# Half of the in-place scans of a selective-scan kernel take their decays from SBUF in place of PSUM

## The chip, the cores and the metric

The kernel runs on one core of a Trainium2 chip. The metric is the device time of one execution in microseconds (us). Before the change the median of three runs is 11,285.59 us, from 11,276.82 to 11,286.57. The profile comes from one execution of its own, told of below. Engines are named as in the profile: PE (TensorE), PEld (its weight loads), DVE (VectorE), ACT (ScalarE), POOL (GpSimd) and SP (SyncE, which here issues all DMAs).

## The reference, cut to what matters

Eight images of 96 channels, 64 by 64, go through a block with four selective scans, then a small attention and a feed-forward part. The scans are most of the work. Each of four directions (row order and column order, each forwards and backwards) has 192 channels with 16 states each, and 4,096 positions in a row:

```python
def step(hst, inp):
    u_i, dt_i, b_i, c_i = inp
    dA = jnp.exp(dt_i[..., None] * A)
    hst = dA * hst + (dt_i * u_i)[..., None] * b_i[:, :, None, :]
    y = jnp.einsum('bkdn,bkn->bkd', hst, c_i)
    return (hst, y)
...
return ys.transpose(1, 2, 3, 0) + D[None, :, :, None] * u
```

So each position needs a decay dA (an exponential), an input (a product), the recurrence itself, a product with c and a sum over the 16 states. The four directions' results are added up.

## The kernel before

**Chunks and slots.** A direction of an image is cut into 8 chunks of 512 positions, a "unit"; 8 images x 4 directions x 8 chunks are 256 units, worked one after another. A unit has 192 x 16 rows, which are 24 scans of 128 rows (64 channels with 2 states): six tiles (n = 0 to 5) of four scans (m = 0 to 3). One scan is one "slot", q = 24 x unit + 4n + m.

**One slot.** ACT makes the decay (line 1080) of 128 x 512 in a PSUM bank "da", of which there are three. DVE runs the scan (line 1145) over the decay and the input hb, which POOL made in SBUF (line 959: b times du, four scans in one instruction of 128 x 2048). There are two sorts:
- In a *banked* scan the states go back into the PSUM bank in the decay's place. DVE then multiplies them by c into hb (line 1147), and ACT copies the last column to the carry (line 1148).
- In the others the states go into SBUF, in the input's place, hb. One copy of ACT takes the carries of a whole tile (line 1153), and POOL multiplies the tile's states by c (line 965).

`BANKED` says how many scans of each tile are banked: all four of tiles 0, 2 and 4, none of 1 and 3, and one or two of tile 5. So 10 or 11 of the 24 scans of a unit are in place: slots 4 to 7, 12 to 15 and the last two or three.

**Order.** Every engine takes its instructions in the order in which the program gives them out, slot after slot. `plan` lists what else goes out at each slot: inputs of the tile after next (slots 1, 5, 9, 13, 17, 21), outputs (slots 8 and 16, and slot 0 of the next unit), the step sizes (PE, three of ACT, one of DVE at line 938, one of POOL at line 941), their spreading over partitions by DMA, loads of b and c. `decays(q + 2)` gives out the decay of the scan two slots ahead; three banks hold the decay in use and the two next.

**Sums.** PE adds the 16 states with a constant matrix into two PSUM banks (`sums`, line 985). For the last part it adds what the earlier directions left: `before` (line 967) loads that into the SBUF buffers u0 and u1 at slot 0 of the next unit, and the matmul of line 994 adds it at slot 6. `gather` copies the sums (slots 10 and 11) to buffers yt0 and yt1 and asks for a DMA to DRAM that goes out three slots later.

**Beside the scans** run side streams, given out step by step between the slots: the front part of the next image and the back part of the last one, whose operations are spread over PE, ACT, DVE and, for one add, POOL (line 802). One of DVE's is the scaled identity of line 694, once for each image.

Of the kernel before, what the change touches and what calls it, by code (L numbers as in the profile page):

```python
# [9 lines left out]
F32 = mybir.dt.float32  # L10
F16 = mybir.dt.float16
F8 = mybir.dt.float8e5
AF = mybir.ActivationFunctionType
# [9 lines left out]
T = 512  # L23
NC = L // T
G = 4
# [7 lines left out]

BANKED = ((4, 0, 4, 0, 4, 1), (4, 0, 4, 0, 4, 2))

HOLD = 3
LAND = 11
SETTLE = 12
# [5 lines left out]
def kernel(ctx: ExitStack, tc: tile.TileContext, a, out):  # L44
# [9 lines left out]
    P = 128  # L54
# [6 lines left out]
    BANKS = {"da": 3, "dt": 1, "f0": 1, "f1": 1, "y01": 1, "y2": 1}  # L61

    def bank(tag, name):
        return psum.tile([P, T], F32, tag=tag, name=name, bufs=BANKS[tag])


    ident = wp.tile([P, P], F32, name="ident")
# [39 lines left out]
    def into(t, src):  # L107
        nc.sync.dma_start(t, src)
        return t
# [3 lines left out]
    def later(dst, src):  # L113

        requests.append((clock[0] + HOLD, dst, src))

# [6 lines left out]
    def load(name, shape):  # L123
        return into(wp.tile(shape, F32, name="w_" + name), a[name])
# [31 lines left out]
    a_neg = load("a_logs", [P, 4, 3, 8])  # L156
# [23 lines left out]
    dd_a, dd_b = wp.tile([P, P], F32, name="dd_a"), wp.tile([64, 64], F32, name="dd_b")  # L180
# [170 lines left out]
    def scanned(ap):  # L351
        return ap.rearrange("p (h j i) -> p h j i", h=8, j=8)

    def transposed(ap):

        return ap.rearrange("p (w i j) -> p w j i", w=8, i=8)

    def to_columns(t, c):

        return t.rearrange("d (w h e) -> d h w e", w=8, h=8)[:, c]  # L360

    def by_window(ap):
        return ap.rearrange("p (w e) -> p w e", w=8)
# [453 lines left out]
    def in_turn(stages, k, settle):  # L817

        for stage, cs in stages:
            yield from stage(k, cs)  # L820
            if settle:
                yield from settled()
# [12 lines left out]
    def drained(*streams):  # L835
        while any(s.on for s in streams):
            tick()
            for s in streams:
                s.run()

    def all_issued():
        drained(Stream(iter((HOLD + 1,))))

# [11 lines left out]
    units, images = [], []  # L855
    for b in range(out.shape[0]):
# [3 lines left out]
        for order, (pair, back) in enumerate((p, k) for p in s["pairs"] for k in range(2)):  # L860
            for i in range(NC):
                u = Unit()
# [11 lines left out]
    first = front(0, images[0])  # L874
# [9 lines left out]
    sp = scan_pool.enter_context(tc.tile_pool(name="scan", bufs=2))  # L884
# [70 lines left out]
    def inputs(u, n):  # L955

        g, j = TILES[n]
        hb = u.hb[n] = sp.tile([P, G, T], F32, tag="hb", name="hb", bufs=HB)
        nc.gpsimd.tensor_tensor(hb, u.bc[0, g], u.du[j].unsqueeze(1).to_broadcast([P, G, T]), ALU.mult)  # L959
# [7 lines left out]
    def before(u):  # L967

        src = u.s["y" if u.order else "u"][u.pair]
        u.plain = []  # L970
        for i, rows in enumerate((slice(0, P), slice(P, src.shape[0]))):
            t = sp.tile([P, T], F32, tag=f"u{i}", name=f"u{i}", bufs=1)[: rows.stop - rows.start]
            u.plain.append(into(t, src[rows, bass.ts(u.c, T)]))

    def sums(u, ns, m):

        if ns[0] == 0 and m == 0:
            u.p = (bank("y01", "p01"), bank("y2", "p2"))
        low, up = slice(0, 64), slice(64, P)
        if len(ns) == 2:  # L980
            todo = [(u.p[0][low], ns[0], m), (u.p[0][up], ns[1], m)]
        else:
            todo = [(u.p[1][low], ns[0], 2 * m), (u.p[1][up], ns[0], 2 * m + 1)]
        for ps, n, i in todo:
            nc.tensor.matmul(  # L985
                ps, halves, u.hb[n][:, i, :], start=TILES[n][0] == 0 and m == 0, stop=False, skip_group_check=True
            )
        if ns[-1] == 5 and m == 1:
            first = u.order == 0
            for ps, w, x in (  # L990
                (u.p[0], dd_a if first else ident, u.plain[0]),
                (u.p[1][low] if first else u.p[1], dd_b if first else ident, u.plain[1]),
            ):
                nc.tensor.matmul(ps, w, x, start=False, stop=True, skip_group_check=True)  # L994

    def gather(u, i):

        ps, d = u.p[i], slice(P * i, P * i + P)
        t = sp.tile([ps.shape[0], T], F32, tag=f"yt{i}", name="yt", bufs=1)

        other = (u.pair, 1 - u.pair, u.pair, 0)[u.order]
        dst = u.s["y"][other][d]
        if other != u.pair:
            nc.scalar.copy(transposed(t), scanned(ps))
            later(to_columns(dst, u.c), by_window(t))
        else:
            nc.scalar.copy(t, ps)
            later(dst[:, bass.ts(u.c, T)], t)
        if u.order == 3 and i == 1:
            if other == u.pair:  # L1010
                u.s["done"].add(u.c)
            elif u.c == (0 if u.back else NC - 1):
                u.s["done"].update(range(NC))

    def plan(u, last, nxt, third):
# [6 lines left out]
        if last:  # L1022
            put(0, outputs, last, 5)
            put(0, before, last)
            for m in range(2):
                put(m, sums, last, (3, 4), 2 + m)
            for m in range(2):
                put(5 + m, sums, last, (5,), m)
            put(7, states, u, 1, 1)
            put(10, gather, last, 0)  # L1030
            put(11, gather, last, 1)
# [38 lines left out]
    def at_index(i):  # L1070
        return units[i] if 0 <= i < len(units) else None

    def decays(q):

        if q >= 24 * len(units):
            return
        u, (n, m) = units[q // 24], divmod(q % 24, G)
        g, j = TILES[n]
        da[q] = bank("da", "da")
        nc.scalar.activation(  # L1080
            da[q], u.delta[j], AF.Exp, scale=a_neg[:, u.k, j, g * G + m : g * G + m + 1]
        )

    da, kept, side, carry = {}, [], [], None
# [13 lines left out]
        step_sizes(units[1:2], i)  # L1098
    inputs(units[0], 0)
    inputs(units[0], 1)  # L1100
    decays(0)
    decays(1)

    def advance(n):

        tick()
        for st in side[:]:
            st.run()

    for u in units:  # L1110
        last, nxt, third = (at_index(u.i + d) for d in (-1, 1, 2))
        if u.new:
            drained(*side)
            b = u.s["b"]
            side = []
            if b == 0:
                side.append(Stream(behind(kit_2, pairs[3:])))
            else:
                side.append(Stream(chain((SETTLE,), in_turn(back_end(b - 1, last.s), kit_b, False))))
            if b + 1 < out.shape[0]:  # L1120
                side.append(Stream(in_turn(front(b + 1, images[b + 1]), kit_f, True), PACE))
            else:
                final = back_end(b, u.s)
                last_kit = back_kit(None, "f0", True, kit_f)
                side.append(Stream(final[0][0](last_kit, range(1, NC)[::-1])))
        if u.i == pairs[3] - 2:
            drained(side[0])
        if third and third.new:
            drained(*side[-1:])
            all_issued()  # L1130
        if u.start:
            carry = sp.tile([P, 24], F32, tag="carry", name="carry")
        todo = plan(u, last, nxt, third)
        for slot in range(24):
            n, m = divmod(slot, G)
            g, j = TILES[n]
            q, hb, first_at = 24 * u.i + slot, u.hb[n], 0 if u.back else T - 1
            col = carry[:, 8 * j + g * G + m : 8 * j + g * G + m + 1]
            while kept:
                kept.pop(0)()  # L1140
            decays(q + 2)
            d = da.pop(q)
            banked = m < u.banked[n]
            dd, x = (d[:, ::-1], hb[:, m, ::-1]) if u.back else (d, hb[:, m, :])
            nc.vector.tensor_tensor_scan(dd if banked else x, dd, x, 0.0 if u.start else col, ALU.mult, ALU.add)  # L1145
            if banked:
                nc.vector.tensor_tensor(hb[:, m, :], d, u.bc[1, g][:, m, :], ALU.mult)  # L1147
                kept.append(lambda col=col, d=d, at=first_at: nc.scalar.copy(col, d[:, at : at + 1]))  # L1148
            elif m == G - 1:
                lo = 8 * j + g * G  # L1150
                kept.append(
                    lambda c=carry[:, lo + u.banked[n] : lo + G].unsqueeze(2), h=hb[:, u.banked[n] :, :], at=first_at:
                    nc.scalar.copy(c, h[:, :, at : at + 1])  # L1153
                )
            for f, args in todo[slot]:
                f(*args)
            place[0] = slot
            advance(slot)
# [7 lines left out]
    for m in range(2):  # L1166
        sums(u, (5,), m)
    gather(u, 0)
    gather(u, 1)
    all_issued()  # L1170
# [77 lines left out]
```

## Time and profile before

| | us | where from |
|---|---|---|
| median of three runs | 11,285.59 | times |
| the profiled execution | 11,276.69 | times |
| its span, first to last instruction | 11,274.7 | profile |
| first scan starts | 299.2 | trace |
| last scan ends | 11,035.9 | trace |
| POOL: inputs of the scans, line 959, 1,536 of them | 6,938.6 | groups |
| POOL: outputs, line 965, 768 of them | 2,984.6 | groups |
| DVE: scans into PSUM, line 1145, 3,087 with a carry | 3,950.2 | groups |
| DVE: scans in place, line 1145, 2,289 with a carry | 2,781.6 | groups |
| DVE: products of the banked scans, line 1147, 3,528 | 2,440.8 | groups |
| ACT: decays, line 1080, 6,144 | 4,216.2 | groups |

How to read it: the first part of the profile's page gives each engine's busy time, the share of the span and the number of instructions. The second cuts the span into 40 slices and gives each slice's busy share in tenths (9 is 90% or more). A row of the groups has the line, the engine, the operation, what it writes and reads, the shape and the count; then the busy time in us and the mean of one in ns; then the idle time of the engine just before these instructions, and what ended it. A row of the waits has who waited for whom, the total in us, how many times, and the longest. A row of the timeline has the start and the duration in us.

### The profile page before, as it was taken

How to read it: one execution, taken by the hardware profiler on the slowest of the kernel's cores; microseconds unless marked ns; L12 is line 12 of the kernel's file. 1: busy time of each engine (PE TensorE's matmuls, PEld its weight loads, DVE VectorE, ACT ScalarE, POOL GpSimd, SP SyncE). 2: the span in 40 equal slices, each digit the busy share in tenths (PEclk: the TensorE clock that was granted, in tenths of full speed). 3: DMA queues.
4: the chain of work that ended last, by engine and by line, in shares of the span. 5: the costliest groups of instructions: out<-in, count | busy, mean ns of one | idle time of the engine just before them, and what ended most of it. 6: DMA issues, size and time to landing. Idle time of an engine off the chain costs nothing. (4 is left out here: it accounts for less than half of the span.)

```text
span 11274.7 us, 97032 instructions
## 1 busy us (share of the span) xinstructions
PE 8525.3 (76%) x23270; PEld 2313.7 (21%) x23270; DVE 10391.9 (92%) x10868; ACT 7482.6 (66%) x14899; POOL 10398.6 (92%) x2782
## 2 busy tenths in 40 slices
PE   6677668887788877888678886788767887676677
PEld 1121112222122211222112221222212221111112
DVE  0999999999999999999999999999999999999993
ACT  2666666767666676667766676666766667666674
POOL 0999999999999999999999999999999999999991
PEclk8787778888788877889788887888878887777778
DMA  3788888988888888888888888889888888888883
GB/s 76 195 200 196 200 190 208 215 219 203 199 208 214 217 194 210 208 210 219 195 208 212 213 215 193 217 200 226 209 199 209 213 221 199 194 198 196 202 201 91
DMA packets 1095376, 2253.25 MB, mean 200 GB/s; under 512 B 435993, under 2 KB 436698, under 8 KB 963731
## 3 DMA queue, kind: packets, MB, share of 16 engines
q1 hardware_dynamic: 1094803, 2247.05, 82.1%
q8 instruction: 184, 3.01, 0.1%
q14 instruction: 389, 3.19, 0.1%
HBM read 1507.14 MB, written 336.69 MB: 164 GB/s over the span
## 5 line engine op out<-in xcount | busy, mean ns | idle before, releaser
L959 POOL TENSOR_TENSOR hb<-b,du 128x2048 f32<-128x2048 f32 x1536 | 6938.6, 4535 | 27.0 <-DMA du<-ua 17.0
L1080 ACT ACTIVATE da<-delta,w_a_logs 128x512 f32<-128x512 f32 x6144 | 4216.2, 689 | 693.1 <-DVE hb L1145 570.8
L985 PE MATMUL p<-hb,halves 128*64 128x512 f32 x12288 | 3788.4, 724 | 787.4 <-POOL hb L965 368.5
L1145 DVE TENSOR_TENSOR_SCAN da<-da,carry,hb 128x512 f32<-128x512 f32 x3087 | 3950.2, 1280 | 52.8 <-ACT da L1080 48.9
L965 POOL TENSOR_TENSOR hb<-hb,c 128x2048 f32<-128x2048 f32 (+2 forms) x768 | 2984.6, 3886 | 296.8 <-ACT carry L1153 252.9
L1145 DVE TENSOR_TENSOR_SCAN hb<-da,carry,hb 128x512 f32<-128x512 f32 x2289 | 2781.6, 1265 | 63.6 <-ACT da L1080 62.6
L1147 DVE TENSOR_TENSOR hb<-da,c 128x512 f32<-128x512 f32 x3528 | 2440.8, 692 | 153.9 <-DVE da L1145 0.5
L1148 ACT COPY carry<-da 128x1 f32<-128x1 f32 x3528 | 554.8, 157 | 2337.9 <-DVE hb L1147 2327.3
L985 PEld LDWEIGHTS p<-hb,halves 128*64 128x64 f32 x12288 | 911.3, 161 | 3513.9 <-issue 2095.9
L435 PE MATMUL conv<-f0im,taps 97*128 97x512 f32 (+1 forms) x2088 | 913.0, 670 | 93.3 <-ACT f0pre L491 54.0
L1145 DVE TENSOR_TENSOR_SCAN da<-da,hb 128x512 f32<-128x512 f32 x441 | 537.7, 1219 | 28.3 <-POOL hb L959 27.3
L941 POOL TENSOR_TENSOR ua<-nat,ua 128x512 f32<-128x512 f32 x256 | 327.4, 1279 | 203.0 <-DMA ub<-u 203.0
L924 PE MATMUL dt<-dts,dt_w 7*64 7x512 f32 (+1 forms) x1024 | 451.1, 662 | 15.8 <-DVE nat L938 12.6
L994 PE MATMUL p<-u,ident 128*128 128x512 f32 x768 | 436.2, 695 | 8.8 <-DMA u<-y 8.8
L938 DVE SCALAR_TENSOR_TENSOR nat<-dt,nat 128x512 f32<-128x512 f32 x384 | 259.6, 676 | 184.4 <-ACT nat L936 184.4
L435 PEld LDWEIGHTS conv<-f0im,taps 97*128 97x128 f32 (+1 forms) x2088 | 256.2, 175 | 683.5 <-issue 523.9
L1145 DVE TENSOR_TENSOR_SCAN hb<-da,hb 128x512 f32<-128x512 f32 x327 | 377.9, 1204 | 4.9 <-ACT da L1080 4.9
L376 PE MATMUL ctr<-f1e,cen_c 96*96 96x512 f32 x402 | 234.7, 693 | 137.4 <-DVE f1e L770 98.6
L382 PE MATMUL var<-f1e,ones_c 96*96 96x512 f32 x350 | 210.8, 687 | 146.3 <-ACT f1e L379 131.7
L619 PE MATMUL cab<-f1im,cab_w 97*32 97x512 f32 x1044 | 272.3, 642 | 14.7 <-DVE f1pad L598 7.8
L1153 ACT COPY carry<-hb 128x4 f32<-128x4 f32 (+2 forms) x768 | 146.8, 191 | 196.1 <-DVE hb L1145 184.1
L656 PE MATMUL cab<-f1m,cab_w 96*96 96x512 f32 x348 | 205.2, 717 | 93.1 <-ACT f1e L665 42.1
(427 smaller groups left out, 7512.6 us busy)
## 6 DMA issues: line engine op xcount, KB each, us to landing
b<-xd SPq DMA_DIRECT2D x1024, 512.0 KB
c<-xd SPq DMA_DIRECT2D x1024, 512.0 KB
delta<-nat SPq DMA_DIRECT2D x1536, 128.0 KB
du<-ua SPq DMA_DIRECT2D x1024, 128.0 KB
y<-yt SPq DMA_DIRECT2D x512, 256.0 KB
u<-y SPq DMA_DIRECT2D x384, 256.0 KB
ua<-u SPq DMA_DIRECT2D x256, 256.0 KB
du<-ub SPq DMA_DIRECT2D x512, 128.0 KB
```

The lines of the kernel that those rows point to most:

```text
L435: nc.tensor.matmul(ps, taps[:, t, lo : lo + n], im[:, r0 + dy : r0 + dy + 8, dx : dx + HW], start=t == 0, stop=t == 8,)
L619: nc.tensor.matmul(ps[at : at + 32, :], cab1_w[:, t, :], k.im.t[:, 8 * q + dy : 8 * q + dy + 8, dx : dx + HW], start=t == 0, stop=t == 8, ...
L924: nc.tensor.matmul(ps, dt_w[32 * w.k : 32 * w.k + R + 1, d], w.dts, start=True, stop=True)
L941: nc.gpsimd.tensor_tensor(x, u.nat, x, ALU.mult)
L959: nc.gpsimd.tensor_tensor(hb, u.bc[0, g], u.du[j].unsqueeze(1).to_broadcast([P, G, T]), ALU.mult)
L965: nc.gpsimd.tensor_tensor(hb, hb, u.bc[1, TILES[n][0]][:, lo:, :], ALU.mult)
L985: nc.tensor.matmul(ps, halves, u.hb[n][:, i, :], start=TILES[n][0] == 0 and m == 0, stop=False, skip_group_check=True)
L994: nc.tensor.matmul(ps, w, x, start=False, stop=True, skip_group_check=True)
L1080: nc.scalar.activation(da[q], u.delta[j], AF.Exp, scale=a_neg[:, u.k, j, g * G + m : g * G + m + 1])
L1145: nc.vector.tensor_tensor_scan(dd if banked else x, dd, x, 0.0 if u.start else col, ALU.mult, ALU.add)
L1147: nc.vector.tensor_tensor(hb[:, m, :], d, u.bc[1, g][:, m, :], ALU.mult)
L1148: kept.append(lambda col=col, d=d, at=first_at: nc.scalar.copy(col, d[:, at : at + 1]))
```

## The change

The decays of the in-place scans with even m go into a new SBUF tile "das" with two buffers: slots 4, 6, 12, 14 and 22, in both rows of `BANKED`. They are 5 of the 24 decays of a unit, 1,280 of 6,144. All others stay in the three PSUM banks. `ahead` holds two lists of the decays still to make, one for PSUM and one for SBUF, each in the scans' order. At each slot q, `decays(q)` gives out from each list as many as there is room for (three in PSUM, two in SBUF, with the one in use counted) and as lie at most eight slots ahead.

To make room, the buffers yt0 and yt1 go away: `gather` copies the sums into u0 and u1, which held what was just added. `before` now keeps whole tiles of 128 rows, of which the first direction uses the lower 64 for the second bank.

```diff
+AHEAD = 8
...
-            t = sp.tile([P, T], F32, tag=f"u{i}", name=f"u{i}", bufs=1)[: rows.stop - rows.start]
-            u.plain.append(into(t, src[rows, bass.ts(u.c, T)]))
+            t = sp.tile([P, T], F32, tag=f"u{i}", name=f"u{i}", bufs=1)
+            into(t[: rows.stop - rows.start], src[rows, bass.ts(u.c, T)])
+            u.plain.append(t)
...
-                (u.p[1][low] if first else u.p[1], dd_b if first else ident, u.plain[1]),
+                (u.p[1][low], dd_b, u.plain[1][low]) if first else (u.p[1], ident, u.plain[1]),
...
-        ps, d = u.p[i], slice(P * i, P * i + P)
-        t = sp.tile([ps.shape[0], T], F32, tag=f"yt{i}", name="yt", bufs=1)
+        ps, d, t = u.p[i], slice(P * i, P * i + P), u.plain[i]
...
+    ahead = ([], [])
+    for q in range(24 * len(units)):
+        n, m = divmod(q % 24, G)
+        ahead[int(m >= units[q // 24].banked[n] and m % 2 == 0)].append(q)
+
     def decays(q):
 
-        if q >= 24 * len(units):
-            return
+        for which, room in ((0, BANKS["da"]), (1, 2)):
+            while ahead[which] and sum(used == which for _, used in da.values()) < room:
+                nxt = ahead[which][0]
+                if nxt > q + AHEAD:
+                    break
+                ahead[which].pop(0)
+                decay(nxt, which)
+
+    def decay(q, which):
+
         u, (n, m) = units[q // 24], divmod(q % 24, G)
         g, j = TILES[n]
-        da[q] = bank("da", "da")
+        da[q] = bank("da", "da") if which == 0 else sp.tile([P, T], F32, tag="das", name="das"), which
         nc.scalar.activation(
-            da[q], u.delta[j], AF.Exp, scale=a_neg[:, u.k, j, g * G + m : g * G + m + 1]
+            da[q][0], u.delta[j], AF.Exp, scale=a_neg[:, u.k, j, g * G + m : g * G + m + 1]
         )
...
-    decays(0)
-    decays(1)
+    decays(-1)
...
-            decays(q + 2)
-            d = da.pop(q)
+            decays(q)
+            d, _ = da.pop(q)
```

## The prediction

> **What bounds the kernel now.** I read the page's busy times first, then its slices, the groups, the waits, and last the timeline around one odd instruction.
>
> ```profile
> PE 8525.3 (76%) x23270; PEld 2313.7 (21%) x23270; DVE 10391.9 (92%) x10868; ACT 7482.6 (66%) x14899; POOL 10398.6 (92%) x2782
> DVE  0999999999999999999999999999999999999993
> POOL 0999999999999999999999999999999999999991
> ```
>
> DVE and POOL are both full from the second slice to the next to last. The first scan starts at 299.2 us and the last ends at 11035.9, so 10,737 us hold the 256 chunks, 41.95 each. In that stretch DVE is busy 10,316 and POOL 10,372: idle 421 and 365 us. Neither can lose or gain much without the other.
>
> ```profile
> L959 POOL TENSOR_TENSOR hb<-b,du 128x2048 f32<-128x2048 f32 x1536 | 6938.6, 4535 | 27.0 <-DMA du<-ua 17.0
> L1080 ACT ACTIVATE da<-delta,w_a_logs 128x512 f32<-128x512 f32 x6144 | 4216.2, 689 | 693.1 <-DVE hb L1145 570.8
> L1145 DVE TENSOR_TENSOR_SCAN hb<-da,carry,hb 128x512 f32<-128x512 f32 x2289 | 2781.6, 1265 | 63.6 <-ACT da L1080 62.6
> L965 POOL TENSOR_TENSOR hb<-hb,c 128x2048 f32<-128x2048 f32 (+2 forms) x768 | 2984.6, 3886 | 296.8 <-ACT carry L1153 252.9
> ```
>
> POOL's work is long multiplies, each with two SBUF inputs. The waits that more decays ahead could remove are small:
>
> ```profile
> DVE hb L1145 <- ACT da L1080: 67.5, 93, 3.0
> DVE da L1145 <- ACT da L1080: 48.9, 22, 6.4
> ```
>
> 116 us in 115 waits: the most that the look-ahead itself can win.
>
> **What the change puts at stake.** Until now every two-input DVE operation of the scan phase has one tensor in PSUM. The change gives 5 scans of each 24 (slots 4, 6, 12, 14, 22), 1,280 in all, both tensors in SBUF. No row shows that beside POOL, so I bound it by the nearest ones:
>
> ```profile
> L1145 DVE TENSOR_TENSOR_SCAN hb<-da,carry,hb x2289: 1250/1260/1285, 346.2 to 11034.7; 128x512 f32<-128x512 f32 x191
> L667 DVE TENSOR_REDUCE totals<-f1e x58: 655/672/683, 2201.7 to 11154.5; 96x1 f32<-96x512 f32 x58
> L694 DVE TENSOR_SCALAR dgate<-ident,gate x8: 268/2484/2492, 2300.0 to 11160.0; 96x96 f32<-96x96 f32 x8
> ```
>
> These columns are least, median and most ns. A scan with one SBUF input never stretches beside POOL (1250 to 1285), nor does a reduction with one SBUF stream (655 to 683). The scaled identity of line 694, SBUF to SBUF, takes 268 ns once POOL has finished and about 2,484 the seven times POOL works. The timeline, DVE's row first and POOL's below, shows why:
>
> ```profile
> 2299.99 2.48 DVE L694 TENSOR_SCALAR dgate<-ident,gate 96x96 f32<-96x96 f32 x1
> 2302.40 1.21 DVE L1145 TENSOR_TENSOR_SCAN hb<-da,hb 128x512 f32<-128x512 f32 x1
> ...
> 2293.42 8.99 POOL L959 TENSOR_TENSOR hb<-b,du 128x2048 f32<-128x2048 f32 x2
> ```
>
> POOL ends at 2302.41, line 694 at 2302.47. All seven end 63 to 70 ns behind a POOL multiply: DVE stood still until POOL's whole instruction was over. So one end is "as L667": no cost. The other is "as L694": each changed scan waits for the multiply in flight. I take L694, because the changed scan draws a second SBUF stream, one more than any row shows running freely; both ends stay in the range.
>
> The Trainium skill, page "SBUF — State Buffer", section "Who interferes with whom", speaks against this change: a DVE instruction with two SBUF inputs contends with a GpSimd instruction that reads SBUF, and whoever comes second is blocked for the whole instruction. L694 agrees with the blocking (2,484 against 268 ns), while two SBUF inputs are not in this trace. By that rule the sum below stands; without it, the free-scan rival's.
>
> **The sum, stage by stage.** POOL's queue per chunk is: after slot 23 an output (L965), an input (L959), the 128x512 multiply of L941, an input; after slot 7 an output and two inputs; after slot 15 the same. Each output waits for the four scans of its tile. Pitches, start to start: L959 and the full L965 4.49 (two in 8.99 to 9.05, less one of 4.53), L941 1.23, the short L965 2.55 on average (200 of 2.31, 56 of 3.41), in-place scan 1.22 (four in 4.80 to 4.92). From a tile's last scan to its output on POOL at the earliest: 0.74 (0.66 to the end of the carry copy of L1153, mean of 768, and 0.08 on). Line 694 needs 268 ns alone but ends at most 70 ns behind POOL, so POOL lets go about 0.2 before its recorded end: DVE gets in between two back-to-back multiplies, and POOL then waits for the scan.
>
> Stage A (slot 23's scan to slot 7's, today 13.76). Slot 4's scan comes 13.76 − 4 × 1.22 = 8.88 into it. POOL's gap before its last input is at 0.74 + 2.55 + 4.49 + 1.23 − 0.2 = 8.81. In the trace 43% come later. Early: scan to 10.03, input to 14.52, slot 6's scan starts at 14.32, and with slot 7's ends at 16.76. Late: it waits for the last input, 13.30, and four scans end at 18.18, without a further wait as POOL has run dry. Mean 17.37, +3.61.
>
> Stage B (to slot 15, today 13.69). Gap at 0.74 + 2 × 4.49 − 0.2 = 9.52; 22% come later. Early 9.52 + 1.22 + 4.49 − 0.2 + 2.44 = 17.47, late 0.74 + 13.47 − 0.2 + 4.88 = 18.89. Mean 17.78, +4.09.
>
> Stage C (to slot 23, today 14.50). Only slot 22 changes: 0.74 + 13.47 − 0.2 + 2 × 1.22 = 16.45, +1.95.
>
> Sum 9.65 us a chunk, × 256 = 2,470. POOL becomes late by this and then waits for DVE; the stages hold both. The rest, at nothing:
> - Look-ahead: the 116 us lie inside stages that POOL's queue now ends. Without that cover it is −116.
> - Decays: still 6,144 activations, 1,280 into SBUF. Nearest rows: SBUF to SBUF 617 (L934) and 709 (L936) against 689, so −92 to +26 us on ACT, which is idle 3,433 us in the phase.
> - Scan reading SBUF for PSUM: the only sign is 1282 against 1260 when the output moves so. Up to −28 us, covered as above; no row shows a loss.
> - Sums copied into u0/u1: the same 512 copies (578 and 1,091 ns). New is that the load of line 973 waits on SP for the write out of that buffer; behind it are dts, the spreads and the states. From the write's issue to the next such load lie 16 us (median of 510); the longest issue of such a write was 4.53. I take 0. If it were 4.5 late at each column-wise chunk (72), 324 us on SP, still under the five slots until the sums read it.
>
> The profiled run took 11,276.7 us (span 11,274.7), 9 under the median 11,285.6. 11,277 + 2,470 = 13,747, rounded to **13,750**.
>
> **Rivals.**
> - *POOL wins every gap* (8%). Back-to-back multiplies overlap by some 45 ns in the timeline, which speaks for it; L694's early release against. Then A is always 18.18, B 18.89, C 16.45: 53.52, +11.57 × 256 = 2,962, **14,240**. With today's leftovers of POOL's instruction at slots 4, 12, 22 (1.11, 2.02, 2.70) and 3.27 at 6 and 14 simply added, 12.37 × 256 gives 14,440, my upper end.
> - *Only POOL waits, or both share finely* (14%). L694's wait is DVE's, against it; but that operation is another kind. 1,280 × 1.25 = 1,600 on POOL, less its 365 idle at best: **12,510 to 12,880**.
> - *Free scans* (13%, the other side). The second stream costs nothing, as L667; then the 116 us of decay waits and the 28 go, and POOL's idle of 365 leaves room: 11,133 to 11,277, say **11,190**. It decides as soon as the wait per changed scan is under 116 / 1,280 = 0.09 us. A page of the skill leans this way: "Perfetto Trace Analysis", section "Optimizing Scalar/DVE Operations", has about 60 ns of access overhead for DVE on SBUF and 125 on PSUM; by it, as an estimate, another 83 us, unseen here.
> - *The change does not get ahead* (3%, no change). Against: slot 12's decay is issued at slot 5, slot 28's at 20, when their delta has long been there.
>
> My forecast keeps 62%. **Range** 12,500 to 14,450: from POOL-only waiting to the added leftovers. It leaves out the free scans, the no-change case and a few per cent beyond. Differences under 0.2% (23 us) can't be told from none. Slower 0.62 + 0.08 + 0.14 = 0.84, same 0.03, faster 0.13.
>
> **What would show it.** The 1,280 scans with SBUF decays should have a median of several us and end with a POOL multiply, while scans from PSUM keep 1.26 to 1.28; POOL's share in the scan phase falls to some 78% (10,372 of 13,208), or stays near 90% if its blocked time is recorded as busy, with idle before L965 for the carry; DVE's waits for decays vanish. If the new scans take 1.2 us and POOL's multiplies stretch to 5.7, POOL alone pays. If neither stretches, I am wrong.

## The result, and the profile after

The changed kernel takes 13,759 us in the median of four runs (13,757 to 13,768), against 11,282 for the kernel before in four runs: a ratio of 1.2197, 95% interval 1.2176 to 1.2218. The forecast was 13,750. The profiled execution took 13,760.1 us with a span of 13,758.4.

The page of the changed kernel, busy times and two rows of slices:

```profile
PE 9199.2 (67%) x23270; PEld 2431.8 (18%) x23270; DVE 13020.8 (95%) x10868; ACT 7572.5 (55%) x14899; POOL 10816.5 (79%) x2782
DVE  1999999999999999999999999999999999999994
POOL 1888888888888888888788888888878888888872
```

DVE looks busier than ever: 13,021 us in place of 10,392 for the same 10,868 instructions. That is not work: as the groups show, the wait sits inside the durations of the changed scans. POOL fell from 92% to 79%. The groups of the changed kernel:

```profile
L960 POOL TENSOR_TENSOR hb<-b,du 128x2048 f32<-128x2048 f32 x1536 | 7298.2, 4766 | 18.1 <-DMA du<-ua 16.9
L966 POOL TENSOR_TENSOR hb<-hb,c 128x2048 f32<-128x2048 f32 (+2 forms) x768 | 2975.7, 3875 | 2022.7 <-ACT carry L1167 1879.3
L1159 DVE TENSOR_TENSOR_SCAN hb<-das,carry,hb 128x512 f32<-128x512 f32 x1120 | 3734.7, 3335 | 0.4
L1159 DVE TENSOR_TENSOR_SCAN hb<-da,carry,hb 128x512 f32<-128x512 f32 x1169 | 1466.5, 1255 | 0.8
```

The 1,120 changed scans with a carry take 3,335 ns in the mean, the in-place scans whose decays stayed in PSUM 1,255. All 1,280 changed ones add up to 4,273 us, where the same slots took 1,614 before: 2,659 more, against 2,481 by which the scan phase grew (13,218 for 10,737). POOL's outputs, which hardly waited before (297 us), now stand idle for 2,023 us until a tile is scanned and its carry copied.

The forms of the scan line in the changed kernel (least, median and most ns):

```profile
L1159 DVE TENSOR_TENSOR_SCAN da<-da,carry,hb x3087: 1254/1281/1293, 340.5 to 13511.3; 128x512 f32<-128x512 f32 x193
L1159 DVE TENSOR_TENSOR_SCAN hb<-da,carry,hb x1169: 1248/1251/1284, 351.6 to 13514.4; 128x512 f32<-128x512 f32 x195
L1159 DVE TENSOR_TENSOR_SCAN hb<-das,carry,hb x1120: 1249/3456/8934, 349.1 to 13513.2; 128x512 f32<-128x512 f32 x187
```

Only the form with both tensors in SBUF stretches, and its least is 1249. Of the 192 changed scans under 1.4 us, 187 began with POOL idle or within 0.3 us of the end of its instruction: there the second SBUF tensor costs nothing extra. DVE's timeline in one chunk of the changed kernel:

```profile
6000.85 4.29 DVE L1159 TENSOR_TENSOR_SCAN hb<-das,carry,hb 128x512 f32<-128x512 f32 x1
6005.06 1.25 DVE L1159 TENSOR_TENSOR_SCAN hb<-da,carry,hb 128x512 f32<-128x512 f32 x1
...
6014.58 2.17 DVE L1159 TENSOR_TENSOR_SCAN hb<-das,carry,hb 128x512 f32<-128x512 f32 x1
6016.67 1.25 DVE L1159 TENSOR_TENSOR_SCAN hb<-da,carry,hb 128x512 f32<-128x512 f32 x1
6017.85 4.30 DVE L1159 TENSOR_TENSOR_SCAN hb<-das,carry,hb 128x512 f32<-128x512 f32 x1
```

and POOL's in the same stretch:

```profile
5998.62 5.43 POOL L960 TENSOR_TENSOR hb<-b,du 128x2048 f32<-128x2048 f32 x1
6006.68 4.51 POOL L966 TENSOR_TENSOR hb<-hb,c 128x2048 f32<-128x2048 f32 x1 [2.62 <-ACT carry L1167]
6011.15 9.91 POOL L960 TENSOR_TENSOR hb<-b,du 128x2048 f32<-128x2048 f32 x2
```

POOL's input ends at 5998.62 + 5.43 = 6004.05, the scan that began at 6000.85 ends at 6005.14, 1.09 later. The median over each of the five changed slots is 1.08. A scan needs some 1.26, so it gets going 0.18 us before POOL's recorded end. The other direction shows too: 408 of POOL's 1,536 input multiplies last over 5 us, mostly 5.4 in place of 4.5, and 402 of them begin inside a changed scan's recorded time (some 360 us in all, 7,298 against 6,939 in the groups). The 9.91 of the last row are two multiplies, one of them so stretched, with a scan between them.

One multiply does not explain the longest scans (8.93 us in the row above, 9.18 without a carry). In 59 of the 1,280 changed scans, 45 of them at slot 4, two to four of POOL's instructions end inside the recorded time; these scans take 6.23 us in the mean. One such scan, and POOL's instructions in its time:

```profile
5013.12 7.91 DVE L1159 TENSOR_TENSOR_SCAN hb<-das,carry,hb 128x512 f32<-128x512 f32 x1
```

```profile
5008.67 4.50 POOL L960 TENSOR_TENSOR hb<-b,du 128x2048 f32<-128x2048 f32 x1
5013.14 1.15 POOL L803 TENSOR_TENSOR f1e<-f1e,f1o 96x512 f32<-96x512 f32 x1
5014.25 1.26 POOL L942 TENSOR_TENSOR ua<-nat,ua 128x512 f32<-128x512 f32 x1
5015.47 4.49 POOL L960 TENSOR_TENSOR hb<-b,du 128x2048 f32<-128x2048 f32 x1
```

Here POOL keeps its turn at three ends in a row, and the scan ends 1.07 us behind the fourth. Why POOL keeps its turn in some places and DVE gets in at others is not shown.

Means of the three stages in us (from last scan to last scan of tiles 1, 3 and 5, in the traces; they move by 0.01 with the first and last chunk):

| stage | before | forecast | after |
|---|---|---|---|
| A, to slot 7 | 13.76 | 17.37 | 17.45 |
| B, to slot 15 | 13.69 | 17.78 | 17.34 |
| C, to slot 23 | 14.50 | 16.45 | 16.87 |
| a chunk | 41.95 | 51.60 | 51.66 |

### The profile page after: what moved, and what is told of

The parts are those of the page before. It is cut to its first block, busy times and chain, and to the rows that moved or that the text cites. A ratio compares the mean times of both kernels' runs of the same rounds, so it can differ in the third digit from the quotient of the medians.

```text
span 13758.4 us, 96349 instructions
## 1 busy us (share of the span) xinstructions
PE 9199.2 (67%) x23270; PEld 2431.8 (18%) x23270; DVE 13020.8 (95%) x10868; ACT 7572.5 (55%) x14899; POOL 10816.5 (79%) x2782
## 5 line engine op out<-in xcount | busy, mean ns | idle before, releaser
L960 POOL TENSOR_TENSOR hb<-b,du 128x2048 f32<-128x2048 f32 x1536 | 7298.2, 4766 | 18.1 <-DMA du<-ua 16.9
L987 PE MATMUL p<-hb,halves 128*64 128x512 f32 x12288 | 4055.3, 771 | 1201.3 <-POOL hb L966 536.7
L1095 ACT ACTIVATE da<-delta,w_a_logs 128x512 f32<-128x512 f32 x4864 | 3356.9, 691 | 1169.4 <-DVE hb L1159 1057.6
L1159 DVE TENSOR_TENSOR_SCAN hb<-das,carry,hb 128x512 f32<-128x512 f32 x1120 | 3734.7, 3335 | 0.4
L1095 ACT ACTIVATE das<-delta,w_a_logs 128x512 f32<-128x512 f32 x1280 | 915.3, 715 | 1557.0 <-DVE hb L1159 1555.1
L1159 DVE TENSOR_TENSOR_SCAN hb<-da,carry,hb 128x512 f32<-128x512 f32 x1169 | 1466.5, 1255 | 0.8
L436 PE MATMUL conv<-f0im,taps 97*128 97x512 f32 (+1 forms) x2088 | 987.2, 728 | 227.2 <-ACT f0pre L492 111.3
L925 PE MATMUL dt<-dts,dt_w 7*64 7x512 f32 (+1 forms) x1024 | 493.2, 716 | 74.8 <-DVE nat L939 71.5
L1159 DVE TENSOR_TENSOR_SCAN hb<-das,hb 128x512 f32<-128x512 f32 x160 | 538.2, 3364 | 0.0
L942 POOL TENSOR_TENSOR ub<-nat,ub 128x512 f32<-128x512 f32 x128 | 162.0, 1266 | 407.9 <-DVE nat L939 378.3
```

The lines of the kernel that those rows point to most:

```text
L436: nc.tensor.matmul(ps, taps[:, t, lo : lo + n], im[:, r0 + dy : r0 + dy + 8, dx : dx + HW], start=t == 0, stop=t == 8,)
L925: nc.tensor.matmul(ps, dt_w[32 * w.k : 32 * w.k + R + 1, d], w.dts, start=True, stop=True)
L942: nc.gpsimd.tensor_tensor(x, u.nat, x, ALU.mult)
L987: nc.tensor.matmul(ps, halves, u.hb[n][:, i, :], start=TILES[n][0] == 0 and m == 0, stop=False, skip_group_check=True)
L1095: nc.scalar.activation(da[q][0], u.delta[j], AF.Exp, scale=a_neg[:, u.k, j, g * G + m : g * G + m + 1])
```

## The experiments

Experiments 1, 11 and 12 have several runs and an interval, the others a single run each; between single runs, differences of a fifth of a per cent are not read.

**1. The shared sum buffers alone.** The decays stay as before. This part of the change is kept, with the whole tiles of `before` that it needs:

```diff
-        ps, d = u.p[i], slice(P * i, P * i + P)
-        t = sp.tile([ps.shape[0], T], F32, tag=f"yt{i}", name="yt", bufs=1)
+        ps, d, t = u.p[i], slice(P * i, P * i + P), u.plain[i]
```

> The part of the change that copies the sums into u0 and u1, alone; all decays stay in PSUM as before. My theory (the whole loss is DVE's wait for POOL at the scans with two SBUF inputs): no difference, 11,282 within 25 us, POOL and DVE both some 97% busy in the scan phase. Rival (SP is held up by the load that now waits for the write out of the same buffer): up to 324 us more, 11,300 to 11,600, with waits of SP at the load of u.

Measured: 11,284 us in ten runs, ratio 1.000, interval 0.999 to 1.001. The load that waits for the write costs nothing. All of the loss lies in the decays.

**2. and 3. What POOL reads.** In the changed kernel and in the kernel before, POOL's input and output multiplies become memsets, so both kernels leave the products with b, du and c out:

```diff
-        nc.gpsimd.tensor_tensor(hb, u.bc[0, g], u.du[j].unsqueeze(1).to_broadcast([P, G, T]), ALU.mult)
+        for _ in range(2):
+            nc.gpsimd.memset(hb, 0.5)
...
-        nc.gpsimd.tensor_tensor(hb, hb, u.bc[1, TILES[n][0]][:, lo:, :], ALU.mult)
+        for _ in range(2):
+            nc.gpsimd.memset(hb, 0.5)
```

> The changed kernel with each of POOL's input and output multiplies (lines 960 and 966) replaced by two memsets of the same tile, which read nothing from SBUF; the inputs of the scans are then a constant, and the products with b, du and c are left out. From the 128x528 memset of 0.53 us I estimate 4.1 us for the two, so POOL is nearly as busy as before. Theory (it is the second SBUF stream that collides with POOL's reads): changed scans of 1.25 us beside POOL's memsets, a few longer ones beside the multiplies of line 942, time 11,050 to 11,300. Rival (DVE waits whatever POOL does, as it would if the write side collided too): changed scans of 2 to 5 us, time above 12,000. The Trainium skill, page SBUF - State Buffer, section Who interferes with whom, says of two-SBUF-input DVE instructions that they contend with a GpSimd instruction that reads SBUF, not with one that only writes it; by that the first of the two holds.

> The same memsets in the kernel before, as the control of the changed kernel with memsets: POOL's multiplies by b, du and c are left out. DVE bound, 11,050 to 11,300. The difference between the two is what the look-ahead and the SBUF decays are worth by themselves when nothing collides: by the 116 us of waits for decays, the changed one is 0 to 150 us faster than this one.

Measured: 11,287 us with the change, 11,279 without. The changed scans with memsets beside them, and then the group of those memsets:

```profile
L1161 DVE TENSOR_TENSOR_SCAN hb<-da,carry,hb x1169: 1247/1258/1284, 342.4 to 11038.1; 128x512 f32<-128x512 f32 x195
L1161 DVE TENSOR_TENSOR_SCAN hb<-das,carry,hb x1120: 1250/1274/3267, 341.2 to 11036.9; 128x512 f32<-128x512 f32 x187
```

```profile
L961 POOL MEMSET hb<- 128x2048 f32 x3072 | 5514.5, 1805 | 115.1 <-PE p L989 26.5
```

POOL works for 8,371 us of the scan phase, less than the 10,372 before but still 78% of it, and writes the same buffers, yet the median changed scan takes 1,274 ns. The collision is with POOL's *reads*. The few long ones, up to 3.3 us, are 15% of those at slot 4, where POOL's queue still has the multiply of the step sizes, which reads. The Trainium skill, page "SBUF — State Buffer", section "Who interferes with whom", says this of instructions with two SBUF inputs, and the run agrees: 3,335 ns beside reading multiplies, 1,308 beside memsets, in the mean.

The pair gives two more answers. The look-ahead and the SBUF decays were expected to be worth 0 to 150 us where nothing collides; no gain is measured (11,287 against 11,279, too close to tell apart). Some collisions are left, though: the scans at the five slots add up to 1,659 us with the change and 1,613 without, nearly all of the 46 us at slot 4. Less these, the change could be worth some 40 us at most, as an estimate. And POOL had been 97% busy in the scan phase before, but with 2,000 us of its work gone the time stays 11,279: POOL does not set it. DVE, busy 10,298 of the phase's 10,728 us there, is the nearest bound.

**4. and 5. The length of the instruction in flight.** POOL's inputs in two halves, in the changed kernel and in the one before:

```diff
-        nc.gpsimd.tensor_tensor(hb, u.bc[0, g], u.du[j].unsqueeze(1).to_broadcast([P, G, T]), ALU.mult)
+        for h in (slice(0, 2), slice(2, 4)):
+            nc.gpsimd.tensor_tensor(
+                hb[:, h, :], u.bc[0, g][:, h, :], u.du[j].unsqueeze(1).to_broadcast([P, 2, T]), ALU.mult
+            )
```

> The changed kernel with each of POOL's input multiplies split into two of 128x1024. The instruction in flight is then at most some 2.3 us long. My theory (a changed scan waits for the whole instruction in flight): the changed scans fall to a mean near 2.1 us, the longest mostly under 3.7, and the time to 12,100 to 12,600, although POOL has more instructions. Rival (a price of the scan itself, or of bytes moved in SBUF): scans stay at 3.3 us and the time at 13,760 or above, by POOL's 0.13 us for each split.

> The same split in the kernel before, as the control. No scan there has two SBUF inputs, so only POOL's second instruction counts: 2 x 2.31 - 4.49 = 0.13 us for each of 1,536, 200 us at most: 11,280 to 11,480 under every theory, scans unchanged at 1.25 to 1.28 us.

Measured: 12,651 us with the change, 11,328 without. The changed scans with halved inputs:

```profile
L1162 DVE TENSOR_TENSOR_SCAN hb<-das,carry,hb x1120: 1251/2132/9349, 354.6 to 12407.5; 128x512 f32<-128x512 f32 x187
```

The median falls from 3,456 to 2,132 and the time by 1,108 us, though POOL has 1,536 more instructions: the price is mostly the multiply in flight. The time is 50 above the range and the mean of all changed scans 2.45 in place of 2.1. The theory left out the scans that sit through more than one end of POOL's instructions: they are 122 of 1,280 here and take 5.48 us in the mean, while the others take 2.12, as forecast. It also left out POOL's own waits: its halves last 2,670 ns here and 2,383 without the change, 882 us in all, and POOL is full again (11,644 us busy, 463 idle in the phase).

In the kernel before with halves, line 694 shows the same wait: 0.46 to 0.48 us in place of 2.48, seven times, each time ending 0.06 to 0.07 behind one half, with the next half right behind it.

**6. One changed scan a chunk.**

```diff
-        ahead[int(m >= units[q // 24].banked[n] and m % 2 == 0)].append(q)
+        ahead[int(n == 5 and m == 2)].append(q)
```

> Only the decay of slot 22 in SBUF, one scan a chunk in place of five. My theory: stage C (slot 15 to 23) is ended by POOL's queue and takes 16.5 to 16.9 us as in the changed kernel, stages A and B stay near 13.8 and 13.7: 11,277 + 256 x (16.87 - 14.50) = 11,884, between 11,700 and 11,950. Rival (reading two SBUF inputs is slow in itself, the same for each scan): the scan has a fixed length near 3.3 us with little spread, time 11,277 + 2,475 / 5 = 11,772.

Measured: 11,972 us, 22 above the range. Stages A and B are 13.68 and 13.77, as expected; C is 17.22. The scan is far from a fixed length:

```profile
L1159 DVE TENSOR_TENSOR_SCAN hb<-das,carry,hb x224: 1274/4214/6516, 384.6 to 11729.4; 128x512 f32<-128x512 f32 x112
```

One scan of the five costs 684 us, more than a fifth of 2,475: POOL's output comes 1.82 us after slot 15's scan in place of 1.25 in the changed kernel, so everything behind it is later, and slot 22's scan meets the last input in the median 1.2 us after its start, with 3.3 us of it still to run (1.8 and 2.7 in the changed kernel).

**7. and 8. The same number of scans at two places.** Slots 4, 6, 12 and 14, and then slots 6, 7, 14 and 15:

```diff
-        ahead[int(m >= units[q // 24].banked[n] and m % 2 == 0)].append(q)
+        ahead[int(n in (1, 3) and m in (0, 2))].append(q)
```

> The decays of slots 4, 6, 12, 14 in SBUF, slot 22 back in PSUM: four changed scans a chunk, each with an unchanged one between. My theory (each changed scan waits for POOL's whole multiply in flight, and POOL's queue then ends the stage): stages A and B as in the changed kernel (17.45 and 17.34), C as before (14.50): 11,277 + 256 x (3.69 + 3.65) = 13,156, between 13,000 and 13,300. Rival (a scan with two SBUF inputs has a fixed price wherever it stands): 11,277 + 4/5 x 2,475 = 13,257. This run alone does not tell them apart, it is the control of the pairs.

```diff
-        ahead[int(m >= units[q // 24].banked[n] and m % 2 == 0)].append(q)
+        ahead[int(n in (1, 3) and m in (2, 3))].append(q)
```

> As many changed scans as the control with even slots, four a chunk, but at slots 6, 7, 14 and 15, two behind each other. My theory (the second of a pair finds POOL stopped or dry, so a pair waits once): A 0.74 + 2.55 + 4.49 + 1.23 + 4.49 - 0.2 + 2.44 = 15.74, B 14.01 + 2.44 = 16.45, C 14.50: 46.69 x 256, that is 11,277 + 1,213 = 12,490, between 12,300 and 12,750; slots 7 and 15 mostly at 1.25 us. Rival (fixed price per scan): the same as the control, about 13,200.

Measured: 13,267 us for the even slots, inside the range, with stage A at 17.84 (forecast 17.45), and 12,829 for the pairs. The same 1,024 scans cost 438 us less when they stand in pairs, so there is no fixed price per scan. Slots 7 and 15 are under 1.4 us in 94 and 96% of the chunks: the second of a pair hardly ever waits, as was forecast. But the pairs are 79 us above their range. Stage B is 16.36 (forecast 16.45) and C 14.41, while A is 17.20 in place of 15.74. In that run the carry copy behind slot 23 ends 1.92 us after its scan, where I had counted 0.66, and POOL's output starts at 2.01.

**9. The pairs without the look-ahead.** The same edit, and

```diff
-AHEAD = 8
+AHEAD = 2
```

> The pairs (slots 6, 7, 14, 15) once more, with AHEAD = 2. The pairs with AHEAD = 8 took 12,829 in place of 12,490; their stage A was 17.20 in place of 15.74, with the carry copy behind slot 23 ending 1.92 us after its scan where I had counted 0.66. My theory (decays made eight slots ahead stand on ACT in front of that copy, and POOL's output waits for it): the copy ends some 0.3 us after the scan, stage A falls to 15.4 to 15.8 and the time to 12,350 to 12,520. Rival (the stage is long for another reason, the pair's own waits): 12,830 within 60 us.

Measured: 12,569 us, 260 less than with eight ahead. The copy now ends 0.79 after slot 23's scan and stage A is 16.31. The time and stage A lie above their ranges. The copy fell to 0.79 and not to 0.3, and POOL's output starts 1.04 after the scan where the sum had 0.74; this explains 0.30 of stage A's 0.57 above 15.74, and the rest stays open. The rival's 12,830 is ruled out: most of the surplus was the look-ahead.

**10. and 11. The look-ahead of the change itself,** AHEAD = 2 with all five slots, a single run and then four:

> The changed kernel with AHEAD = 2: the SBUF decays are made at most two scans ahead, as all decays were before. My theory: nothing changes but the few waits for decays: 13,760 within 1%, changed scans again near 3.3 us on average. Rival (the new order of ACT's work, with decays far ahead of the copies and side work, costs the time): most of the 2,475 us comes back, below 12,500.

> The changed kernel with AHEAD = 2 once more, timed for an interval: one look gave 13,664 against 13,759. My theory (made far ahead, decays delay the carry copies, mean 0.58 us from scan to copy's end against 0.30 with AHEAD = 2, and POOL's outputs with them): the ratio to the kernel before is 1.210 to 1.215, below the changed kernel's 1.2197. Rival (look-ahead has no effect either way): 1.2197 within its interval of 1.2176 to 1.2218.

Measured: 13,664 us in the single run; 13,663 in the four, ratio 1.2108, interval 1.2088 to 1.2128, below the changed kernel's and clear of it. The changed scans are nearly as long with two ahead as with eight (4,231 us in all, against 4,273). So the look-ahead is not the cause of the loss, and not a gain either: it adds some 96 us. The waits show how. With eight ahead (the first row is ACT's own):

```profile
ACT das L1095 <- DVE hb L1159: 1555.1, 660, 8.2
POOL hb L966 <- ACT carry L1167: 1879.3, 592, 9.5
```

A decay eight slots ahead goes into the buffer that a changed scan is still reading. ACT takes its work in order, so it stands there up to 8.2 us, and the carry copies and other decays stand behind it. With two ahead that wait is no longer among the forty longest, the carry copy comes 0.30 us after its scan in the mean (0.58 with eight), and POOL's output 0.65 after it (0.89).

**12. The one blocked instruction of the kernel before.** The scaled identity of line 694 goes from DVE to ACT:

```diff
-            nc.vector.tensor_scalar(dgate, ident[:C, :C], gate, None, ALU.mult)
+            nc.scalar.activation(dgate, ident[:C, :C], AF.Copy, scale=gate)
```

> The kernel before with the scaled identity of line 694 made by ACT in place of DVE. My theory (that operation blocks DVE for 2.2 us seven times): seven waits less, 7 x 2.2 = 15 us at most, 11,267 within 15 us, barely above what can be told from no change. Rival (DVE's stall there is hidden behind POOL, which is as full): 11,282 within 10 us.

Measured: 11,270 us in eleven runs against 11,288, ratio 0.9983, interval 0.9974 to 0.9992. It takes ACT 374 ns each time:

```profile
L694 ACT ACTIVATE dgate<-ident,gate x8: 374/374/376, 2305.0 to 11152.0; 96x96 f32<-96x96 f32 x8
```

The 18 us (by the interval 9 to 29) agree with the 7 x 2.2 = 15 that were forecast, and the rival's no difference is outside the interval. This version is the only one here that beats both kernels, by a little.

## Why the prediction was right, point by point

- **The row it rested on.** Between "as the reduction" (no wait) and "as line 694" (a wait for POOL's whole instruction) I chose line 694. Shown: the changed scans end 1.08 us behind POOL's multiply, halving the multiply cuts the wait, and taking POOL's reads away ends it. Some luck was in the choice: line 694 reads one tensor and a column of 96 scalars, not two tensors, and which of its properties makes it wait is not shown. It told how long a wait lasts, not that a scan with two SBUF tensors would have it; only the runs show that.
- **DVE gets in between two back-to-back multiplies.** Forecast from line 694, which must have begun 0.2 us before POOL's recorded end. Measured 0.18. In stage B the first scan came before the last input in 96% of the chunks. The rival in which POOL wins every gap (14,240) is out. But DVE does not win every gap either: 59 of the 1,280 scans, mostly at slot 4, sit through two to four ends of POOL's instructions.
- **The stages hold both engines.** Right as a sum, 51.60 forecast and 51.66 measured, but partly by terms that cancel: stage B is 0.44 under its forecast, C 0.42 over. That the time came within 9 us is luck; that it came near is not. In stage B, 4% of the first scans missed POOL's gap and not the 22% of the old trace; POOL's output there starts 0.56 us after slot 7's scan, where it started after 1.17 before. Early ones took 17.24 (forecast 17.47), late ones 20.18 (18.89). In stage A it was 34%, not 43%; early ones took 16.79 (forecast 16.76), late ones 18.70 (18.18).
- **A term left out: the second multiply of the step sizes.** In odd chunks POOL has the one for ub (line 941 before) in front of slot 16's output, and it waits for a DVE step given out at slot 15. POOL stood for that step 55 us in all before, and 378 with the change. Now POOL's output comes 2.01 us after slot 15's scan in odd chunks and 0.48 in even ones, where I had 0.74 for both; stage C is 17.49 and 16.27. The mean of the two is 0.5 above 0.74, which accounts for the +0.42 of stage C.
- **A wait not named: the look-ahead on ACT.** I took the decays as hidden by ACT's idle time. They are in amount, not in order: about 96 us (experiments 10 and 11). DVE's waits for decays, 116 us before, fell to 35 for the PSUM decays and did not vanish, and no gain shows in the time. POOL's share in the scan phase came to 82%, between the two figures that the prediction gave (78 and near 90): part of its blocked time is recorded as busy, the rest as idle.
- **The other edits** at nothing: right, ratio 1.000 (experiment 1).
- **"Neither can lose or gain much without the other"** was half right. POOL could lose 2,000 us of work without any gain (experiment 3), and 212 us more of it cost about 40 (experiment 5). So POOL was not the bound, though close below it.
- **The rivals.** Only POOL waits: out, DVE's scans carry 2,659 us. Free scans: out here. With POOL's reads mostly gone 11,287 was measured and not 11,190; without the 46 us of collisions left in that run it would be some 11,240, as an estimate.

## What to carry to other kernels

Before an operand of a DVE instruction is moved from PSUM to SBUF, count how many tensors it then reads from SBUF, and look at what POOL reads meanwhile: here the price was what was left of POOL's instruction, so it fell when POOL's instructions were halved (the size of DVE's was not varied). Look in the old trace for a DVE instruction on SBUF whose longest time is far above its least, and lay it beside POOL's timeline; here seven executions of a 0.27 us instruction, though not of quite the same kind, told what a wait of 1,280 others would cost. Making operands further ahead is only free if the buffer they go into is free at that moment, since an in-order engine that waits for it holds up all that is queued behind.

## What the runs showed of the hardware that was not expected

- A blocked DVE instruction is recorded as busy, and so is a blocked POOL instruction (5.4 us for 4.5). DVE's share rose from 92% to 95% while it did the same work.
- A scan that reads both tensors from SBUF is no faster than one that reads the decay from PSUM. At the same slots beside memsets, with the change and without, the medians differ by 2 ns at most (slot 12: 1,275 and 1,274; slot 14: 1,258 both). The 1,274 and 1,258 in the rows of experiment 3 differ by the slots that they hold.
- Line 694's instruction, still on DVE in the changed kernel, takes 265 to 268 ns all eight times there: each time POOL stands idle, seven times since 1.3 us or a little more, waiting for the tile that DVE has just scanned. Its stall went away without being touched.
